# Cross-attention scores with tokens in partitions, probabilities transposed through DRAM, loads in half chunks

## The chip, the cores and the metric

The kernel runs on one core of a Trainium2 chip. The metric is the device time of one execution in microseconds. The core has TensorE (PE; the profile lists its weight loads as PEld), VectorE (DVE), ScalarE (ACT), GpSimd (POOL) and SyncE (SP), each with its own instruction stream, and DMA engines that move data between the on-chip memory (SBUF) and DRAM. Matmuls write to PSUM, which the code divides into banks of 128 x 512 floats.

## The reference

Sixteen sequences of 128 tokens with 512 features go through one block: cross-attention to a context of 2048 rows (without weights), causal self-attention with 16 heads, and a mixture of two of eight low-rank experts chosen by the first token.

```python
def xattn(h, ctx):                       # h: (16, 128, 512), ctx: (16, 2048, 512)
    scores = einsum('bld,bvd->blv', h, ctx)
    probs = softmax(scores, axis=-1)
    return einsum('blv,bvd->bld', probs, ctx)

x = x + xattn(layernorm(x), ctx)
x = x + attn(layernorm(x), Wq, Wk, Wv, Wc)     # 16 heads, rope, causal
x = x + experts(layernorm(x), Wr, A, Bw)       # top 2 of 8, gates from token 0
```

Everything is in float32.

## The kernel before

The program is unrolled over the 16 batches (sequences). For every batch there are four generators, `score`, `attend`, `inner` and `experts`; each `yield` ends one step, and a loop over `b` calls `step(...)` so that the steps of neighbouring batches interleave: while batch `b` is in self-attention (`inner`), the cross-attention of `b + 1` (`attend`) and the scores of `b + 2` (`score`) run, and the experts of `b - 1`. The order on TensorE and the order of the DMAs of `load` are as the program writes them (`keep_in_program_order`); instructions on the other engines may be reordered by the scheduler unless they are `pinned`. The last two batches end in a list, `CLOSING`, that is kept in order on every engine.

All compute instructions of DVE, ACT and POOL pass through one helper and carry the line L115; matmuls are L137, transposes on TensorE L140, pinned DMAs L145. So rows are told apart by tile names.

`score(b)` normalizes `x`, turns it (`hT1`, features in partitions), and multiplies with the transposed context `ctxT`. The context comes in four chunks of 512 rows (VC = 4), each as a transposed copy `ctxT` and a plain copy `ctx`, 1 MB a chunk and copy. With the context chunk as the stationary operand and `hT` as the moving one, the scores `psc` have context rows in partitions: 16 products of 128 x 128 a chunk, four chunks. In float32 the trace has two passes for a product. The maximum over all rows is then one over partitions: elementwise maxima (`mx`), a transpose on TensorE (`tr_m`), a reduction (`nm`), a diagonal matrix (`diag`), a product with ones that spreads it to all partitions (`spread`), four additions on DVE, and four exponentials on ACT. The sums of the probabilities are added up on DVE (`sums`, `part`), and `den` is a product with ones. The probabilities lie as `attend(b)` needs them: context rows in partitions, as the stationary operand against `ctx` (`av`), 16 products of 128 x 512. `x1` is `av` times the inverse sum plus `x`.

`inner(b)` makes v, k and q, the head scores (`pss`), the probabilities in four groups of four heads (`weigh`: mask, peaks, exponentials, scaling), and transposes them by a way through DRAM: DVE transposes blocks of 32 x 32 into `pX`, `send` writes them to DRAM, `fetch` reads them back in the other order into `pT`, from where `y` and then `o` take them. `x2` is `o` plus `x1`. The same way is used for the normalized rows of `score`, `inner` and `experts` (`blocks_1`, `blocks_2`, `blocks_3` to `hT`). All sends and fetches are issued from SP, in program order.

The loads of the loop are issued from ACT's stream, four whole chunks of `ctx` of batch `b + 2` in one place and four of `ctxT` of `b + 3` in another. Each of the two has four buffers, so a chunk's buffer comes free when the chunk of the batch before has been read. PSUM banks: two for scores (`sc`), three for accumulation (`acc`), three for transposes (`tr`).

Of the kernel before, what the change touches and what calls it, by code (L numbers as in the profile page):

```python
# [48 lines left out]
pss0.14 av1.15 m1.14 m0.14 share.13 mx1.14 rx.13 e1.14 lg.13 fold.15 av2.15 choose.13 mx0.14  # L49
ga.13 last_fold.15 e0.14 n1.14 den.15 av3.15 ex.13 n0.14 gb.13 rden.15 gate.13 wa.13 pss1.14  # L50
# [39 lines left out]
def perceiver_block(ctx: ExitStack, tc: tile.TileContext, io: dict, out: bass.AP):  # L90
# [133 lines left out]
    def send(name):  # L224
        if name in ways:
            blocks, dst = ways[name]
            each = blocks.shape[2] * QD
            there = dram.tile([P, 4 * each], F32, tag=f"there_{each}", name=f"there_{name}")
            load(there, blocks.rearrange("p q n j -> p (q n j)"))
            ways[name] = there, dst  # L230

    def fetch(name):
        if name in ways:
            there, dst = ways.pop(name)
            load(
                dst.rearrange("p a n j -> p a (n j)"),
                there.rearrange("(a i) (q e) -> (i q) a e", a=4, q=4),
            )

# [21 lines left out]
    def transposed(src, dst, name, by_tensor):  # L261
        n = src.shape[1] // P
        if by_tensor:
            for piece in tensor_pieces(lambda: src, dst, name, n):
                piece()
        else:
            blocks = p1.tile([P, 4, n, QD], F32, tag=f"blocks_{name[0]}", name=f"blocks_{name}")
            vector.transpose(blocks, src.rearrange("p (n q i) -> p q n i", n=n, q=4))
            ways[name] = blocks, dst
# [74 lines left out]

    def load_ctx(b, vs=range(VC)):
        for v in vs:
            t = p4.tile([P, 4, D], F32, tag="ctx", name=f"ctx_{b}_{v}")

            load(
                t, io["ctx"][b, v * 512 : (v + 1) * 512].rearrange("(p j) d -> p j d", j=4),  # L350
                queue=queue,
            )
            cts.setdefault(b, []).append(t)

    def first_norm(x, hT):

        stats = const.tile([P, 6], F32, name="st_first")
        mv, rstd = const.tile([P, 2], F32, name="mv_first"), const.tile([P, 1], F32, name="rs_first")
        vector.bn_stats(stats, x)
        vector.bn_aggr(mv, stats)  # L360
        pinned(gpsimd.tensor_scalar_add(rstd, mv[:, 1:2], EPS))
        gpsimd.tensor_tensor(rstd, rstd, mhalf, ALU.pow)
        h = p2.tile([P, D], F32, tag="h", name="h_1_0")
        for c in range(KC):

            tr = bank(ps_tr, "tr", f"tr_1_0_{c}") if c else bank(ps_acc, "acc", "tr_1_0_0")
            at = slice(c * P, (c + 1) * P)
            vector.tensor_scalar(
                mixed(h)[:, c], plain(x)[:, c], mv[:, 0:1], rstd, ALU.subtract, ALU.mult
            )  # L370
            transpose(tr[:, :P], h[:, at], ident)
            scalar.copy(hT[:, :, c, :], tr[:, :P].rearrange("p (a j) -> p a j", a=4))
            warm_up(1)


    def score(b):

        hT = p1.tile([P, 4, KC, QD], F32, tag="hT1" if b != 1 else "hT3", name=f"hT1_{b}")
        if b:
            h = layernorm(xs[b], f"1_{b}", mix=b == 1)  # L380
            yield
            transposed(h[:], hT, f"1_{b}", b == 1)
        else:
            first_norm(xs[b], hT)
            yield
        yield

        sc = p2.tile([P, VC, 4, S], F32, tag="sc", name=f"sc_{b}")
        mx = p1.tile([P, 4, S], F32, tag="mx", name=f"mx_{b}")
        for v, ct in enumerate(turned_cts.pop(b)):  # L390
            ps = bank(ps_sc, "sc", f"psc_{b}_{v}").rearrange("p (j t) -> p j t", j=4)
            for j in range(4):

                if v == VC - 1 and j == 3:
                    yield
                for c in range(KC):
                    matmul(
                        ps[:, j, :].rearrange("p (a i) -> p a i", a=4),
                        ct[:, c, j * P : (j + 1) * P], hT[:, :, c, :],
                        start=(c == 0), stop=(c == KC - 1),  # L400
                    )
            scalar.copy(sc[:, v], ps)

            if v:
                vector.tensor_tensor(mx, ps, mx if v > 1 else sc[:, 0], ALU.max)
            if v < VC - 1:
                yield

        def halved(t, op):
            vector.tensor_tensor(t[:, :2], t[:, :2], t[:, 2:], op)  # L410
            vector.tensor_tensor(t[:, 0], t[:, 0], t[:, 1], op)
            return t[:, 0]

        most = halved(mx, ALU.max)
        yield

        tr = bank(ps_tr, "tr", f"tr_m_{b}")
        transpose(tr[:, :S], most, ident)
        nm = p2.tile([P, 1], F32, tag="nm", name=f"nm_{b}")
        vector.tensor_reduce(nm, tr[:, :S], AX.X, ALU.max, negate=True)  # L420
        diag = p1.tile([P, S], F32, tag="diag", name=f"diag_{b}")
        vector.tensor_scalar(diag, ident, nm, None, ALU.mult)
        yield
        spread = bank(ps_tr, "tr", f"spread_{b}")
        matmul(spread[:, :S], ones, diag, start=True, stop=True)
        for v in range(VC):
            vector.tensor_tensor(
                sc[:, v], sc[:, v], spread[:, None, :S].to_broadcast([P, 4, S]), ALU.add
            )
            scalar.activation(sc[:, v], sc[:, v], AF.Exp)  # L430
        part = p2.tile([P, S], F32, tag="part", name=f"part_{b}")
        scores[b] = (sc, part)
        yield
        sums = p1.tile([P, 4, S], F32, tag="sums", name=f"sums_{b}")
        pinned(vector.tensor_tensor(sums, sc[:, 0], sc[:, 1], ALU.add))
        yield
        for v in range(2, VC):
            pinned(vector.tensor_tensor(sums, sums, sc[:, v], ALU.add))

        def fold():  # L440
            vector.tensor_tensor(sums[:, :2], sums[:, :2], sums[:, 2:], ALU.add)

        def last_fold():
            vector.tensor_tensor(part, sums[:, 0], sums[:, 1], ALU.add)

        if b == B - 1:
            named(b, fold=fold, last_fold=last_fold)
        else:
            fold()
            last_fold()  # L450
        yield

    def attend(b):

        sc, part = scores.pop(b)
# [3 lines left out]
        def quarter(v):  # L459
            for j in range(4):  # L460
                matmul(
                    acc, sc[:, v, j, :], ct[v][:, j, :],
                    start=(v == 0 and j == 0), stop=(v == VC - 1 and j == 3),
                )

        state = {}

        def whole():
            den = state["den"] = bank(ps_tr, "tr", f"den_{b}")
            matmul(den[:, :1], part, ones[:, :1], start=True, stop=True)  # L470
# [3 lines left out]
        def inverse():  # L474
            vector.reciprocal(rden[:], state["den"][:, :1])
# [6 lines left out]
        if b == B - 1:  # L482
# [3 lines left out]
                den=whole, rden=inverse, x1=added,  # L486
# [6 lines left out]
        for v in range(VC):  # L493
            quarter(v)
            if v == (VC - 1 if b else VC - 2):
                whole()
                inverse()
# [6 lines left out]
    def inner(b):  # L504
# [167 lines left out]
        def held(chunks=every):  # L672
            acc = banks["y", chunks.start].rearrange("p (c t) -> p c t", c=HC)
            scalar.copy(yT[:, chunks, :], acc[:, chunks, :])
# [98 lines left out]
    def routing(b):  # L773
# [7 lines left out]
            p1, [P, TOP, KC * R], tag="each" if b < B - 1 else "mx", name=f"each_{b}"  # L781
# [54 lines left out]
    def early(b):  # L836
# [22 lines left out]
        row = Later(p1, [P, D], tag="sums", name=f"row_{b}")  # L859
# [12 lines left out]
        def share():  # L872
# [6 lines left out]
            v0s=lambda: summed("v0", "blocks_1"), v0t=value,  # L879
# [9 lines left out]
    def experts(b):  # L889
# [57 lines left out]
        def result(cols=slice(0, D)):  # L947
            vector.tensor_tensor(res[:, cols], banks[cols.start][:, cols], res[:, cols], ALU.add)
# [63 lines left out]
    step(score, 0)  # L1012
    step(score, 1)
    load_weight("v")
    load_weight("k")
    step(attend, 0)
    step(score, 0, 2)
# [5 lines left out]
    step(score, 1)  # L1023
# [15 lines left out]
    for i, n, g in halves:  # L1039
        folded = fold_products(i, n, g)  # L1040
        if ready:
            fold_turned(*ready)
        ready = (n, g, folded)
# [5 lines left out]
    queue = nc.scalar  # L1049
    for b in range(B - 2):  # L1050
        if b + 3 < B:
            load_x(b + 3)
        step(inner, b)
        step(experts, b - 1)
        send(f"3_{b - 1}")
        fetch(f"3_{b - 1}")
# [3 lines left out]
        step(inner, b, 3)  # L1060
        step(score, b + 1, 2)
# [3 lines left out]
        step(inner, b, 2)  # L1065
        step(experts, b - 1)
        step(attend, b + 1)
        step(inner, b)
        step(attend, b + 1)
        step(experts, b - 1)  # L1070
        step(inner, b)
        step(experts, b - 1)
        step(inner, b + 1)
        send(f"p_{b}_0")
        fetch(f"p_{b}_0")
        send(f"p_{b}_1")
        send(f"2_{b + 1}")
        fetch(f"p_{b}_1")
        fetch(f"2_{b + 1}")
        step(score, b + 2, 2)  # L1080
        step(score, b + 3)
        step(score, b + 2)
        load_ctx(b + 2)
        step(score, b + 2)
        step(experts, b - 1)
        step(score, b + 2)
        step(experts, b - 1)
        step(inner, b)
        step(inner, b + 1)
        if b + 3 < B:  # L1090
            load_turned(b + 3)
        step(score, b + 2)
        step(score, b + 3)
        step(inner, b)
        step(score, b + 2)
# [8 lines left out]
    step(score, z, 2)  # L1104
# [54 lines left out]
```

## Time and profile before

| | |
|---|---|
| time, median of 3 runs | 810.63 us (810.39 to 810.79) |
| the profiled execution's own time | 810.97 us |
| its span, first to last instruction | 809.2 us |
| PE busy in the span | 800.2 us (99%) |
| PEld busy | 568.5 us (70%) |
| DVE busy | 529.7 us (65%) |
| ACT busy | 260.4 us (32%) |
| POOL busy | 146.6 us (18%) |
| granted TensorE clock, mean | 0.998 |
| moved by DMA | 211.05 MB, mean 261 GB/s |

"Busy" is the time in which an engine had an instruction in work; matmuls overlap each other, so a busy PE isn't the same as a PE at its peak, and the mean duration of one matmul is longer than the distance from one to the next. A group row reads: line, engine, operation, output and inputs, shape, count, then busy time in all and mean ns of one, then the idle time of the engine just before and what ended it. A timeline row reads: start, duration, engine, line, operation, how many instructions were merged.

### The profile page before, as it was taken

Reading aid. Unit: us, or ns where it says so; the run is one execution under the profiler, and the core shown is the slowest. Engines: PE = TensorE matmul, PEld = TensorE weight load, DVE = VectorE, ACT = ScalarE, POOL = GpSimd, SP = SyncE. Lnnn points to the kernel's source line nnn. Section 1 sums busy time; section 2 is a strip of 40 time slices with the busy share of each in tenths; the row PEclk is TensorE's granted clock in tenths of the full one; section 3 lists DMA queues with packets and bytes.
Section 4 is the critical chain, followed back from the end, with each engine's and each line's share of the span. In section 5 each row is a group of like instructions: output and inputs, shape, how many; then the busy total and the mean of one; then the engine's idle time right before and its main releaser. Section 6 shows DMA issues by size and latency. Waiting matters only on the chain.

```text
span 809.2 us, 14363 instructions
## 1 busy us (share of the span) xinstructions
PE 800.2 (99%) x5538; PEld 568.5 (70%) x5538; DVE 529.7 (65%) x1234; ACT 260.4 (32%) x772; POOL 146.6 (18%) x213
## 2 busy tenths in 40 slices
PE   9999999999999999999999999999999999999996
PEld 9946775768677576866758677676867757686653
DVE  2455759386684947658495775938667584856885
ACT  2232324142232423233241232415223241422461
POOL 1001011212121121211112121111212112121204
PEclk9999999999999999999999999999999999999999
DMA  9998394967849497694958859495885949664102
GB/s 375 417 389 321 118 380 171 340 253 251 360 163 381 172 324 292 221 397 142 364 212 292 320 188 399 152 353 222 281 337 181 388 152 340 261 231 173 41 1 79
DMA packets 76868, 211.05 MB, mean 261 GB/s; under 512 B 6400, under 2 KB 42624, under 8 KB 60416
## 3 DMA queue, kind: packets, MB, share of 16 engines
q10 hardware_dynamic: 15696, 113.32, 35.0%
q1 hardware_dynamic: 57168, 84.75, 29.4%
q0 software_dynamic: 3936, 12.07, 4.4%
q8 instruction: 44, 0.72, 0.3%
q14 instruction: 24, 0.20, 0.1%
HBM read 180.23 MB, written 29.88 MB: 260 GB/s over the span
## 4 chain that ended last, share of the span: by engine, by line
PE 97%; DVE 1%; POOL 0%; issue 0%; ACT 0%; POOLq 0%
PE psc L137 28%; PE av L137 28%; PE k L137 7%; PE q L137 7%; PE v L137 7%; PE o L137 6%; PE pss_sc L137 2%; PE y L137 2%; PE ffn L137 2%; PE pss_acc L137 2%; PE mid L137 2%; PE warm L137 1%; PE tr_m L140 0%; PE tr L140 0%; PE spread L137 0%; PE lg L137 0%
## 5 line engine op out<-in xcount | busy, mean ns | idle before, releaser
L137 PE MATMUL psc<-hT,ctxT 128*128 128x128 f32 x2048 | 235.0, 276 | 0.0
L137 PEld LDWEIGHTS psc<-hT,ctxT 128*128 128x128 f32 x2048 | 231.3, 192 | 0.5 <-issue 0.5
L137 PE MATMUL av<-ctx,sc 128*128 128x512 f32 x512 | 227.3, 596 | 0.0
L137 PEld LDWEIGHTS av<-ctx,sc 128*128 128x128 f32 x512 | 94.4, 190 | 110.5 <-issue 107.9
L115 ACT ACTIVATE att<-att,nmx 128x128 f32<-128x128 f32 x256 | 98.8, 388 | 84.9 <-DVE nmx L115 84.9
L115 POOL TENSOR_SCALAR rs<-mv 128x1 f32<-128x1 f32 x47 | 10.6, 225 | 431.0 <-DVE g_at L115 209.5
L115 ACT COPY sc<-psc 128x512 f32<-128x512 f32 x64 | 37.5, 586 | 140.0 <-PE psc L137 140.0
L115 ACT ACTIVATE sc<-sc 128x512 f32<-128x512 f32 x64 | 40.2, 630 | 90.9 <-DVE sc L115 90.4
L137 PE MATMUL k<-hT,w_k 128*128 128x128 f32 x512 | 60.1, 275 | 0.0
L137 PE MATMUL q<-hT,w_q 128*128 128x128 f32 x512 | 60.0, 275 | 0.0
L137 PEld LDWEIGHTS k<-hT,w_k 128*128 128x128 f32 x512 | 58.5, 192 | 1.5 <-issue 0.8
L137 PE MATMUL v<-w_v,hT 128*32 128x512 f32 x520 | 59.0, 593 | 0.0
L137 PEld LDWEIGHTS q<-hT,w_q 128*128 128x128 f32 x512 | 58.5, 192 | 0.0
L137 PE MATMUL o<-w_c,yT 128*128 128x512 f32 x128 | 57.8, 594 | 0.0
L115 DVE TENSOR_TENSOR mx<-psc,mx 128x512 f32<-128x512 f32 x32 | 21.6, 676 | 55.0 <-ACT sc L115 55.0
L115 ACT ACTIVATE kb<-kT,cst 128x512 f32<-128x512 f32 (+1 forms) x34 | 36.2, 1113 | 39.8 <-DVE kT L115 39.8
L115 DVE TENSOR_SCALAR h<-x,mv,rs 128x512 f32<-128x512 f32 x47 | 27.4, 583 | 31.9 <-POOL rs L115 31.9
L115 ACT ACTIVATION_READ_ACCUMULATOR att<-att,nmx 128x1 f32 x256 | 47.9, 187 | 0.0
L115 DVE TENSOR_TENSOR sc<-sc,spread 128x512 f32<-128x512 f32 x64 | 42.6, 671 | 3.3 <-PE spread L137 3.3
L115 DVE TENSOR_TENSOR att<-att,rsm 128x512 f32<-128x512 f32 x64 | 43.4, 678 | 0.8
L115 DVE TENSOR_REDUCE nmx<-att 128x4 f32<-128x512 f32 x64 | 41.8, 671 | 0.1
L137 PEld LDWEIGHTS o<-w_c,yT 128*128 128x128 f32 x128 | 23.9, 196 | 23.8 <-issue 23.0
(139 smaller groups left out, 851.1 us busy)
## 6 DMA issues: line engine op xcount, KB each, us to landing
ctx<-in_ctx_dram ACTq DMA_DIRECT2D x56, 1024.0 KB, 8.4
ctxT<-in_ctxT_dram ACTq DMA_DIRECT2D x52, 1024.0 KB, 10.5
there_p<-pX SPq DMA_DIRECT2D x28, 512.0 KB, 4.0
pT<-there_p SPq DMA_DIRECT2D x28, 512.0 KB, 4.5
ctxT<-in_ctxT_dram SPq DMA_DIRECT2D x12, 1024.0 KB, 8.9
there<-blocks SPq DMA_DIRECT2D x42, 256.0 KB, 3.3
hT<-there SPq DMA_DIRECT2D x42, 256.0 KB, 3.0
ctx<-in_ctx_dram SPq DMA_DIRECT2D x8, 1024.0 KB, 10.5
```

Source lines behind the costliest of these rows:

```text
L115: ins = issue(*args, **kwargs)
L137: tc.keep_in_program_order(nc.tensor.matmul(*args, **kwargs))
```

## The change

The scores are computed the other way round: `hT1` becomes the stationary operand and the `ctxT` chunk the moving one, so that tokens are in partitions and 512 context rows stream in one matmul; a chunk takes four products of 128 x 512. The maximum is a row maximum (`peaks`, then `nm`), and it enters the exponential as a bias; the exponential gives the row sums (`sums`) too. `mx`, `tr_m`, `diag`, `spread`, the additions, `part` and `den` are gone, and two yields of `score` with them.

The probabilities now lie with tokens in partitions and have to be turned for `attend`. From batch 2 on that goes through DRAM as in `inner`: four DVE transposes into `cX0` and `cX1`, two sends, two fetches into `cT0` and `cT1` (512 KB each). Batches 0 and 1 are turned on TensorE, 16 transposes each, and copied by ACT. `hT1` is laid out so that the column of the stationary operand is every fourth float, `cT` so that it is every eighth. `sc` has one buffer instead of two. `blocks_1` shares its buffer with `cX0`. The host orders the columns of `ctxT` to match.

The loads of the loop are cut into halves (512 KB) and spread over the batch, still on ACT's stream; the steps, sends and fetches are placed anew, `x` is loaded one batch further ahead, and the score of batch 1 is finished in the stage that folds the weights. The copy of `yT`, the last addition of the result, `nm` and the exponentials are pinned; `fold`, `last_fold` and `den` leave `CLOSING`.

```diff
@@ send / fetch
-            each = blocks.shape[2] * QD
+            each = blocks.shape[2] * blocks.shape[3]
+    def by_block(t):
+        return t.rearrange("p a j n -> p a n j")
+    def stationary(t, n):
+        return t[:, :, :, n].rearrange("p a j -> p (a j)")
@@ transposed
-            blocks = p1.tile([P, 4, n, QD], F32, tag=f"blocks_{name[0]}", name=f"blocks_{name}")
-            vector.transpose(blocks, src.rearrange("p (n q i) -> p q n i", n=n, q=4))
+            blocks = p1.tile([P, *dst.shape[1:]], F32, tag=f"blocks_{name[0]}" if name[0] != "1" else "cX0", name=f"blocks_{name}")
+            to = blocks if name[0] != "1" else by_block(blocks)
+            vector.transpose(to, src.rearrange("p (n q i) -> p q n i", n=n, q=4))
@@ loads
+    def load_piece(kind, b, v, half):
+        if b >= B:
+            return
+        chunks, tag = ((cts, "ctx"), (turned_cts, "ctxT"))[kind == "T"]
+        if half == 0:
+            t = p4.tile([P, 4, 512], F32, tag=tag, name=f"{tag}_{b}_{v}")
+            chunks.setdefault(b, []).append(t)
+        of = slice(2 * half, 2 * half + 2)
...
+        load(chunks[b][v][:, of, :], src, queue=nc.scalar)
@@ score
-        hT = p1.tile([P, 4, KC, QD], F32, tag="hT1" if b != 1 else "hT3", name=f"hT1_{b}")
+        hT = p1.tile([P, 4, QD, KC], F32, tag="hT1" if b != 1 else "hT3", name=f"hT1_{b}")
-        sc = p2.tile([P, VC, 4, S], F32, tag="sc", name=f"sc_{b}")
+        sc = p1.tile([P, VC, 512], F32, tag="sc", name=f"sc_{b}")
-            for j in range(4):
-                for c in range(KC):
-                    matmul(
-                        ps[:, j, :].rearrange("p (a i) -> p a i", a=4),
-                        ct[:, c, j * P : (j + 1) * P], hT[:, :, c, :],
-                        start=(c == 0), stop=(c == KC - 1),
-                    )
+            for c in range(KC):
+                matmul(ps, stationary(hT, c), ct[:, c, :], start=(c == 0), stop=(c == KC - 1))
             scalar.copy(sc[:, v], ps)
-            if v:
-                vector.tensor_tensor(mx, ps, mx if v > 1 else sc[:, 0], ALU.max)
+            vector.tensor_reduce(peaks[:, v : v + 1], ps, AX.X, ALU.max)
...
+        pinned(vector.tensor_reduce(nm, peaks, AX.X, ALU.max, negate=True))
...
+        for v in range(VC):
+            pinned(scalar.activation(
+                sc[:, v], sc[:, v], AF.Exp, bias=nm, accum_out=sums[:, v : v + 1]
+            ))
+            vector.transpose(
+                by_block(cX[v // 2])[:, :, v % 2 * 4 : v % 2 * 4 + 4, :],
+                sc[:, v].rearrange("p (n q i) -> p q n i", n=4, q=4),
+            )
+            ways[f"c_{b}_{v // 2}"] = cX[v // 2], cT[v // 2]
@@ attend
-                    acc, sc[:, v, j, :], ct[v][:, j, :],
+                    acc, stationary(cT[v // 2], v % 2 * 4 + j), ct[v][:, j, :],
-            vector.reciprocal(rden[:], state["den"][:, :1])
+            vector.tensor_reduce(rden[:], sums, AX.X, ALU.add)
+            vector.reciprocal(rden[:], rden[:])
@@ inner
-            scalar.copy(yT[:, chunks, :], acc[:, chunks, :])
+            pinned(scalar.copy(yT[:, chunks, :], acc[:, chunks, :]))
@@ the loop over b, as it stands after
         step(inner, b)
         step(experts, b - 1)
         send(f"3_{b - 1}")
         step(inner, b)
         if b:
             load_piece("T", b + 2, 2, 0)
             load_piece("T", b + 2, 2, 1)
         fetch(f"3_{b - 1}")
         if b:
             send(f"1_{b + 2}")
             fetch(f"1_{b + 2}")
         step(inner, b, 2)
         step(attend, b + 1)
         step(inner, b)
         step(attend, b + 1)
         step(inner, b)
         load_piece("C", b + 2, 0, 0)
         if b:
             load_piece("T", b + 2, 3, 0)
         step(inner, b)
         load_piece("C", b + 2, 0, 1)
         send(f"p_{b}_0")
         step(experts, b - 1)
         step(attend, b + 1)
         step(inner, b)
         load_piece("C", b + 2, 1, 0)
         if b:
             load_piece("T", b + 2, 3, 1)
         step(attend, b + 1)
         step(experts, b - 1)
         step(inner, b)
         load_piece("C", b + 2, 1, 1)
         fetch(f"p_{b}_0")
         send(f"p_{b}_1")
         step(experts, b - 1)
         load_piece("C", b + 2, 2, 0)
         step(inner, b + 1)
         send(f"2_{b + 1}")
         step(score, b + 2)
         load_piece("C", b + 2, 2, 1)
         fetch(f"p_{b}_1")
         step(score, b + 2)
         load_piece("C", b + 2, 3, 0)
         fetch(f"2_{b + 1}")
         if b + 4 < B:
             load_x(b + 4)
         step(score, b + 3)
         step(score, b + 2)
         load_piece("C", b + 2, 3, 1)
         step(score, b + 2)
         step(experts, b - 1)
         load_piece("T", b + 3, 0, 0)
         step(score, b + 2, 2)
         step(experts, b - 1)
         send(f"c_{b + 2}_0")
         step(inner, b)
         load_piece("T", b + 3, 0, 1)
         send(f"c_{b + 2}_1")
         fetch(f"c_{b + 2}_0")
         step(inner, b + 1)
         load_piece("T", b + 3, 1, 0)
         load_piece("T", b + 3, 1, 1)
         fetch(f"c_{b + 2}_1")
         step(score, b + 3)
         step(inner, b)
```

## The prediction

> **What bounds the kernel now.** I read the page's busy times and the chain of waits first, then the groups of instructions, then TensorE in order of time through one batch of the loop.
>
> ```profile
> PE 800.2 (99%) x5538; PEld 568.5 (70%) x5538; DVE 529.7 (65%) x1234; ACT 260.4 (32%) x772; POOL 146.6 (18%) x213
> ...
> PE 97%; DVE 1%; POOL 0%; issue 0%; ACT 0%; POOLq 0%
> ```
>
> TensorE (PE) is busy 99% of the span, and the chain that ended last is 97% PE: a microsecond less of matmul is a microsecond less of time, as long as nothing arrives late. The waits list shows next to no idle PE in the loop.
>
> ```profile
> L137 PE MATMUL psc<-hT,ctxT 128*128 128x128 f32 x2048 | 235.0, 276 | 0.0
> L137 PEld LDWEIGHTS psc<-hT,ctxT 128*128 128x128 f32 x2048 | 231.3, 192 | 0.5 <-issue 0.5
> L137 PE MATMUL av<-ctx,sc 128*128 128x512 f32 x512 | 227.3, 596 | 0.0
> L137 PEld LDWEIGHTS av<-ctx,sc 128*128 128x128 f32 x512 | 94.4, 190 | 110.5 <-issue 107.9
> ```
>
> The scores (psc) stream 128 columns a pass, the weighted sum (av) 512. Both do the same arithmetic, but psc loads weights back to back (231.3 us), av's weight load idles more than half the time. Durations overlap, so cost is read from start to start:
>
> ```profile
> 397.72 0.33 PE L140 MATMUL tr_m<-ident,mx 128*128 128x128 f32 x1
> 397.89 3.60 PE L137 MATMUL o<-w_c,yT 128*128 128x512 f32 x8
> 401.32 0.39 PE L137 MATMUL spread<-diag,ones 128*128 128x128 f32 x2
> 401.55 3.74 PE L137 MATMUL k<-hT,w_k 128*128 128x128 f32 x32
> ...
> 408.69 3.60 PE L137 MATMUL av<-ctx,sc 128*128 128x512 f32 x8
> 412.22 1.13 PE L137 MATMUL pss_sc<-kb,qT 64*128 64x256 f32 x8
> ...
> 414.15 10.57 PE L137 MATMUL av<-ctx,sc 128*128 128x512 f32 x24
> 424.55 0.28 PE L137 MATMUL den<-ones,part 128*128 128x1 f32 x2
> 424.69 0.37 PE L137 MATMUL lg<-g_part,ones 128*128 128x8 f32 x2
> 424.92 13.64 PE L137 MATMUL psc<-hT,ctxT 128*128 128x128 f32 x120
> 438.40 1.06 PE L137 MATMUL mid<-hT,wa 128*128 128x128 f32 x8
> ```
>
> A batch takes 47.85 us and PE has no hole in it.
>
> [...] That bears on the new stationary operands, 16 bytes (hT1) and 32 bytes (cT) from column to column. No PE row here shows such a load; ScalarE and VectorE show the like:
>
> ```profile
> 409.08 2.37 ACT L115 ACTIVATE kb<-kT,cst 128x512 f32<-128x512 f32 x2 [2.17 <-DVE kT L115]
> 744.11 1.33 ACT L115 ACTIVATE kb<-kT,cst 128x512 f32<-128x512 f32 x2 [2.18 <-DVE kT L115]
> 800.06 1.08 DVE L115 TENSOR_TENSOR res<-x,h 128x512 f32<-128x512 f32 x1
> ```
>
> The first kb reads every fourth float, the second reads in line: 2.37 against 1.33 us, a factor of 1.78. res with one operand read so takes 1.08 us, elsewhere 0.68: 1.59.
>
> **The change on PE, per batch.** Gone: tr_m 0.17 (397.89-397.72), spread 0.23, den 0.14 = 0.54. The scores become 32 passes of 512 columns. Before: 13.48 for 120 passes and 0.89 for the last eight (391.43 to 392.32 a batch earlier) = 14.37. After, priced by av: 3.53+10.40 = 13.93. Saved 0.44; together 0.98. The strided weight load: at best 190 ns, at worst 190x1.78 = 340, both under the 430 of the matmul that covers them, so nothing; without cover each ns over 430 costs 1,024 passes, 1.0 us.
> Batches 2 to 15: 14 x 0.98 = 13.7. Batches 0 and 1 save 1.96 but transpose probabilities on PE: 32 at 0.1275 (the fold transposes, 8 in 1.02) = 4.1; net +2.1. Without stalls 810.97 - 13.7 + 2.1 = 799.4, against the profiled execution (span 809.2 plus 1.8 around it). The median of the runs is 0.3 lower.
>
> **VectorE and ScalarE.** DVE loses four additions of spread, four of sums and the folds, diag (some 6 us a batch). It gains four row maxima (nearest row: nmx reduce, 0.67, as the maxima removed) and four stream transposes, which write at 32 bytes: between 0.70 (pX) and 1.11 (x1.59); I take 0.9. The exponentials take bias and row sum with them: 0.63 plus some 0.06 = 0.69. ACT issues 16 half loads instead of eight whole ones at 0.5 us each, between its exponentials. Neither engine is the bound; what matters is four chains. I put t=0 at k's first matmul; in the new timing av ends at 23.0, psc at 38.0, y starts at 38.96 (second half 39.41), v at 39.86, o at 43.4, the next k at 46.9.
>
> First, x1. In the changed order DVE meets x1 = av*rden+x, which waits for av's end, ahead of the last group's scaling and its transpose into pX; before, x1 came behind them. So DVE stands from about 21 to 23.2. From x1's start to the norm's end took 2.76 us (425.52 to 428.28); then h 0.52, indices 0.40, blocks 0.61, rows and reciprocal 0.30, scaling 0.68, transpose 0.70: pX is ready at 29.2. The send of p_1 and its fetch follow. The page has medians of 4.0 and 4.5 us: landing at 37.8, 1.6 us before y's second half (more on this below).
>
> Second, the first row maximum queues behind that transpose and four gate instructions (0.45): it ends at 30.25. PE wants that bank for psc's third chunk at 30.16. A late bank also exposes part of the 0.19 weight load. Between 0 and 0.5 us a batch; I take 0.25.
>
> Third, the probabilities. psc ends at 38.0; copy 38.8, maximum 39.5, nm 39.7; four exponentials to 42.5; yT's copy behind them to 43.1, just before o at 43.4. Two transposes to 42.3, send 4.0, fetch 4.5: cT at 51, av wants it at 54.0. 3 us to spare.
>
> Fourth, the LayerNorm's blocks_1 now share cX0's buffer and wait for that send (46.3). Queued behind on DVE: x2, its norm, the shuffle of k. o ends only at 46.9, so the wait is nearly covered; kb is ready at 9.4 of the next batch, pss wants it at 10.7.
>
> SP carries four more DMAs a batch (0.37 us each); p_0's send leaves earlier and the loads come in halves over the batch. Bytes: 211 MB plus 28 x 1.05 = 240, 300 GB/s against slices above 410: room, but the sends meet loads:
>
> ```profile
> 422.67 0.32 SPq L145 DMA_DIRECT2D there_p<-pX  x1
> 425.28 0.37 SPq L145 DMA_DIRECT2D pT<-there_p  x1
> 425.76 0.43 SPq L145 DMA_DIRECT2D there_p<-pX  x1
> ...
> 431.54 0.37 SPq L145 DMA_DIRECT2D pT<-there_p  x1
> ```
>
> SP issues a fetch when its send is done: 2.6 us for p_0 alone, 5.8 for p_1 beside other traffic. [...] Beside the send and fetch of p_1 that stretch of 9 us carries two halves of ctx, hT2 both ways, x and the expert gathers, 3.4 MB or 380 GB/s in all, near the full slices. At 5 and 4.9 us the landing falls on 39.2, a hair ahead of y. I take 0.2 us a batch for y waiting.
>
> Sum of stalls: (0.25+0.2) x 13 = 5.9, and 0.5 for the fold stage, where ACT gains four copies and now waits 0.95 of every 2.04 us. 799.4+6.4 = 805.8 profiled, 805.5 for the median.
>
> **Rivals.**
> Slower: y waits for p_1 every batch. At 5.8 for the send (shown above) and 6.0 for the fetch (its longest landing) pT lands at 29.2+5.8+6.0 = 41.0 against 39.41: 1.6 us x 13 = 21, so about 824 with the other stalls. It decides from send plus fetch of 11.2 us, where the stall eats the 0.98. For it: p_1 was slow before; half loads of ctx now fall into that window. Against: the medians sum to 8.5.
> No stall at all: 799. For it: the first three margins are positive or nearly nothing.
> The weight loads are exposed: from a factor of 2.3 on a load (430/190). At 2.5 (475 ns) 46 us more, about 850. Against: 1.78 is the largest factor seen; for: no PE row.
> No effect: 512 columns save nothing with such loads, and stalls take the 0.54: 808 to 812.
> cT late at av: from 3 us beyond the medians, 815.
>
> **How the numbers follow.** Forecast (801 to 809) 0.48; no stall 0.11; y late 0.27; weights exposed 0.05; cT late 0.04; no effect 0.05. Runs of this kernel tell 0.2%, 1.6 us, from nothing. Faster: 0.48+0.11 and a piece of the last, 0.60; within 0.08; slower 0.32. The range runs from 798.5 to 820: it leaves out the exposed weights and the worse half of the late y, 0.19.
>
> **What would show it.** PE's groups: psc 512 passes at 0.43 us start to start; tr_m, spread and den gone; 32 new transposes. PEld's psc and av rows: up to 340 ns is as argued; above 430 is the rival. A wait of psc's load for DVE peaks of 0.1 to 0.3 us a batch; a wait of y for pT's DMA of some tenths. x1 ahead of the last pX on DVE. A batch of about 47.3 us. Wrong would be a batch above 47.85, with the wait that ends last in y, av or pss.

## The result, and the profile after

The changed kernel takes 908.15 us (median of 4 runs, 901.15 to 912.98) against 810.62 us before (4 runs): a ratio of 1.120, 95% interval 1.112 to 1.127. It is slower by 97.5 us. Forecast were 805.5 us, range 798.5 to 820. Runs of one kernel that lie more than 1.5% above its fastest (one of e2 and three of e12 below) are given, but nothing is concluded from them alone.

The page of the changed kernel, busy times and the first line of the chain that ended last:

```profile
PE 829.6 (91%) x3954; PEld 560.8 (62%) x3954; DVE 514.5 (57%) x1130; ACT 279.6 (31%) x844; POOL 145.7 (16%) x213
...
PE 63%; DMA 24%; DVE 8%; issue 2%; POOL 2%; ACT 0%; SPq 0%; POOLq 0%; DVEq 0%
```

PE's passes have fallen from 5538 to 3954, as forecast, but PE is idle for 9% of the span and the chain is 24% DMA, which had no share in it before.

In what follows a trip is a way through DRAM, and its two legs are the send and the fetch. The trip of p is that of the self-attention's probabilities (`pX` to `pT`, in two halves p_0 and p_1), the trip of c that of the cross-attention's (`cX` to `cT`). The groups of v and y before:

```profile
L137 PE MATMUL v<-w_v,hT 128*32 128x512 f32 x520 | 59.0, 593 | 0.0
...
L137 PE MATMUL y<-pT,vv 128*32 128x128 f32 x512 | 17.5, 276 | 0.0
```

The same groups after, and the DMA issues after (KB each, median us from issue to landing):

```profile
L137 PE MATMUL v<-w_v,hT 128*32 128x512 f32 x520 | 79.0, 761 | 4.2 <-DMA hT<-there 4.2
...
L137 PE MATMUL y<-pT,vv 128*32 128x128 f32 x512 | 23.8, 315 | 50.7 <-DMA pT<-there_p 50.7
```

```profile
there_p<-pX SPq DMA_DIRECT2D x28, 512.0 KB, 7.7
pT<-there_p SPq DMA_DIRECT2D x28, 512.0 KB, 7.3
```

y waits 50.7 us for pT (13 waits of 3.9 us on average), nothing before. The two legs of the trip of p take 7.7 and 7.3 us; before, the medians were 4.0 and 4.5. v, unchanged by the diff, takes 79.0 us instead of 59.0. One batch on PE, in order of time, from psc to the next psc:

```profile
419.11 12.62 PE L137 MATMUL psc<-ctxT,hT 128*128 128x512 f32 x28
433.10 1.16 PE L137 MATMUL mid<-hT,wa 128*128 128x128 f32 x8 [1.37 <-POOL wa L115]
...
441.60 0.90 PE L137 MATMUL y<-pT,vv 128*32 128x128 f32 x16 [4.07 <-DMA pT<-there_p]
442.51 4.98 PE L137 MATMUL v<-w_v,hT 128*32 128x512 f32 x32
...
474.35 1.22 PE L137 MATMUL psc<-ctxT,hT 128*128 128x512 f32 x2
```

The batch is 55.24 us (419.11 to 474.35) against 47.85 before. y's second half waits 4.07 us; mid, the experts' first product, waits 1.37 us for the expert weights, which come by a gather from DRAM. And after the wait the matmuls themselves are slow: v takes 4.91 us from start to start, before 3.54. The windows view names it; its columns are window, length, then busy time of PE, PEld, DVE, ACT and POOL, the granted clock, the DMA share and GB/s:

```profile
436.90:441.60 4.70, 0.63 (x17) 0.36 (x17) 3.73 (x6) 2.93 (x8) 0.00 (x0) 1.00 0.97 293
441.60:447.40 5.80, 5.79 (x48) 1.74 (x48) 2.71 (x5) 0.59 (x1) 0.67 (x1) 0.71 0.93 330
```

PE got 0.71 of its clock in the second window, 1.00 in the one before, in which it waited, and in the one after (447.40 to 450.95). So the stall of this batch is paid twice, 4.07 us of waiting and some 1.8 us of slow y and v (e8 and e9 below show the like behind gaps of 2.35 and 2.93 us).

On SP, the trip of p in that batch:

```profile
415.39 0.33 SPq L145 DMA_DIRECT2D there_p<-pX  x1
423.20 0.36 SPq L145 DMA_DIRECT2D pT<-there_p  x1
425.02 0.33 SPq L145 DMA_DIRECT2D there_p<-pX  x1
...
434.90 0.37 SPq L145 DMA_DIRECT2D pT<-there_p  x1
```

A fetch is issued when its send has landed: 7.8 us for p_0, 9.9 us for p_1, and p_1's fetch lands 6.7 us later. The last pX is ready at 424.99, 6.0 us after av's end. On VectorE the order is indeed the one the prediction saw: x1 and the gate stand ahead of the last scaling and pX.

### The profile page after: what moved, and what is told of

It is laid out like the page before. It is cut to its first block, busy times and chain, and to the rows that moved or that the text cites. A ratio compares the mean times of both kernels' runs of the same rounds, so it can differ in the third digit from the quotient of the medians.

```text
span 908.3 us, 11298 instructions
## 1 busy us (share of the span) xinstructions
PE 829.6 (91%) x3954; PEld 560.8 (62%) x3954; DVE 514.5 (57%) x1130; ACT 279.6 (31%) x844; POOL 145.7 (16%) x213
## 3 DMA queue, kind: packets, MB, share of 16 engines
q10 hardware_dynamic: 31248, 113.33, 38.6%
## 4 chain that ended last, share of the span: by engine, by line
PE 63%; DMA 24%; DVE 8%; issue 2%; POOL 2%; ACT 0%; SPq 0%; POOLq 0%; DVEq 0%
PE av L137 25%; DMA there_p<-pX 9%; PE v L137 9%; DMA pT<-there_p 7%; PE k L137 6%; PE q L137 6%; PE o L137 6%; DMA there<-blocks 4%; PE psc L137 3%; DMA hT<-there 3%; PE pss_sc L137 2%; POOL rs L115 2%; PE pss_acc L137 1%; DVE x L115 1%; DVE st L115 1%
## 5 line engine op out<-in xcount | busy, mean ns | idle before, releaser
L137 PE MATMUL psc<-ctxT,hT 128*128 128x512 f32 x512 | 233.1, 608 | 0.8 <-PE lg L137 0.8
L137 PE MATMUL av<-ctx,cT 128*128 128x512 f32 x512 | 230.7, 603 | 0.0
L137 PEld LDWEIGHTS av<-ctx,cT 128*128 128x128 f32 x512 | 158.2, 315 | 56.6 <-issue 4.6
L137 PEld LDWEIGHTS psc<-ctxT,hT 128*128 128x128 f32 x512 | 154.9, 310 | 60.1 <-DVE peaks L115 6.7
L137 PE MATMUL v<-w_v,hT 128*32 128x512 f32 x520 | 79.0, 761 | 4.2 <-DMA hT<-there 4.2
L115 DVE TENSOR_REDUCE peaks<-psc 128x1 f32<-128x512 f32 x64 | 43.9, 687 | 59.1 <-ACT sc L115 59.0
L137 PE MATMUL y<-pT,vv 128*32 128x128 f32 x512 | 23.8, 315 | 50.7 <-DMA pT<-there_p 50.7
L115 DVE STREAM_TRANSPOSE cX<-sc 128x512 f32<-128x512 f32 x56 | 54.5, 1087 | 13.2 <-ACT sc L115 11.3
L137 PEld LDWEIGHTS y<-pT,vv 128*32 128x32 f32 x512 | 13.9, 121 | 65.3 <-DMA pT<-there_p 54.2
L137 PEld LDWEIGHTS v<-w_v,hT 128*32 128x32 f32 x520 | 20.8, 136 | 51.5 <-issue 49.2
```

The costliest lines, as they stand in the source:

```text
L115: ins = issue(*args, **kwargs)
L137: tc.keep_in_program_order(nc.tensor.matmul(*args, **kwargs))
```

## The experiments

All times are medians, except where a single run or a range is given; the runs of one group share their runs of the kernel before (810.6 to 811.0 us).

| run | edit | us |
|---|---|---|
| e1_whole | whole loads at their old places | 921.3 |
| e2_px_first | last pX ahead of x1 | 908.0 (one run) |
| e3_whole_late | e1, but last pX behind x1 | 919.3 |
| e4_no_c_trip | probabilities' trip left out | 908.3 |
| e5_thin_loads | half loads of 128 KB | 805.0 |
| e10_half_bytes | half loads of 256 KB | 810.0 |
| e6_before_halves | kernel before with half loads | 826.0 |
| e7_placed | whole loads, both moved | 929.7 |
| e8_placed_ctxT | whole loads, ctxT moved | 866.3 |
| e9_own_blocks | e8, blocks_1 out of cX0 | 866.7 |
| e11_one_queue | loads in SP's queue | 850.8 |
| e12_one_queue_spread | e11, spread between the legs | 806.6 to 824.6 |
| e13_one_queue_gather | e12, none beside the gather | 806.6 |
| e14_loads_alone | changed kernel with e13's order of loads and trips | 807.0 |

**Loads, order or volume.** The first theory was that the half loads, spread over the batch, slow the trip of p; the rivals were VectorE's order and the added bytes.

```diff
 # e1_whole: as the kernel before has it
-        load_piece("C", b + 2, 0, 0)
...
-        load_piece("T", b + 3, 1, 1)
+        load_ctx(b + 2)                     # after the third copy of psc
+            load_turned(b + 3)              # after the copy of vv
```

> The changed kernel with its loads as before: four whole chunks of ctx and four of ctxT, at the two places of the loop where the kernel before issues them; all else as changed. With other loads the scheduler also puts the last scaling and its transpose into pX ahead of x1 on VectorE, so this run takes away two suspects at once. Theory 'loads' (the half loads, spread into the stretch where the attention probabilities go to DRAM and back, slow that trip) and theory 'order' (x1 ahead of the last pX makes p_1 late) both expect the stall in y to go: a batch of about 47.0 to 47.8 us, 798 to 812 us in all, sends of p of 2.6 to 4.5 us instead of 7.7. Theory 'volume' (the 29 MB that the probabilities add are what slows everything) expects it to stay above 870 us with sends of p above 6 us.

Measured 921.28 us (919.27 to 922.93). 'Loads' and 'order' were wrong about the time, 'volume' had the time but not the sends: the trip of p is fast again (sends of 2.7 and 5.7 us), and the stall has gone elsewhere. PE of this run, then SP:

```profile
412.23 6.15 PE L137 MATMUL av<-ctx,cT 128*128 128x512 f32 x8 [7.33 <-DVE qP L115]
```

```profile
393.44 2.20 SPq L145 DMA_DIRECT2D there_c<-cX  x2
403.48 4.23 SPq L145 DMA_DIRECT2D cT<-there_c  x2
```

av stands still for 7.33 us. The profile names qP on DVE, which ended 0.35 us earlier, but av doesn't read it; in five other batches it names the landing of cT, and in e3 below DVE was done with q 3 us before av went on. So what comes last is taken to be cT, whose first send took 10 us (393.44 to 403.42). That is the stretch of the old loads: from 384 to 408 DMA is busy all the time (a share of 1.00 to 1.05). The kernel before put its loads where no trip of p lay. The change puts a trip of its own there. (ACT's fourth load of ctxT also left 18 us after its first in this run, about when cT landed, and held kb; no run isolates that.)

```diff
 # e2_px_first: program order, with order edges on VectorE
-        step(attend, b + 1)      # q3 and x1
-        step(experts, b - 1)     # logits, gate
-        step(inner, b)           # weigh 3
+        step(attend, b + 1)      # q3
+        step(inner, b)           # weigh 3, last pX
+        step(experts, b - 1)
+        step(attend, b + 1)      # x1
```

> The changed kernel, half loads and all, with one edit: on VectorE the last reciprocal, scaling and transpose into pX stand ahead of x1 and the gate instructions, as they stood before the change; TensorE's order is the same. The last pX is then ready at about 417.3 on the time axis of the changed kernel's trace instead of 424.99. Theory 'order' expects y's wait (4.07 us a batch) and the slow clock behind it (1.8 us) to go in 13 batches: 825 to 840 us. Theory 'loads' expects little: on SP the send of p_1 stands behind the fetch of p_0, which waits for p_0's slow send until 423.2, so p_1 leaves only some 1.4 us earlier: 13 x 1.4 = 18 less, 880 to 900 us.

Measured 908.0 us (a second run took 923.9): no gain over 908.15, and outside both forecasts. The last pX now is ready at 416.9, but SP holds its send:

```profile
413.53 0.33 SPq L145 DMA_DIRECT2D there_p<-pX  x1
421.52 0.36 SPq L145 DMA_DIRECT2D pT<-there_p  x1
421.98 0.46 SPq L145 DMA_DIRECT2D there_p<-pX  x1
```

p_1's send stands behind p_0's fetch, which waits 8 us for p_0's send; its own landing took 10.8 us more. VectorE's order alone brings nothing. Whether p_1's send ahead of p_0's fetch, with the loads left as they are, would help was not tried.

```diff
 # e3_whole_late: e1 with one order edge (shortened)
+            if group == 3:   # scaling of the last group behind x1
+                tc.add_manual_dep(scaled.ins, ahead[b + 1].ins.name, NO_SYNC)
```

> As the run with whole loads at their old places, but on VectorE x1 and the first gate instructions are held ahead of the last scaling and pX, as in the changed kernel, so the last pX comes some 3 to 6 us after av's end. Theory 'loads' expects a trip of 8 to 10 us for p_1 against about 10 us of room: no wait in y or one of a few tenths, 798 to 815 us. Theory 'order' expects most of the loss to come back: 850 us or more.

Measured 919.26 us, 2 us below e1, with av waiting for the c trip as there and no wait in y. So VectorE's order doesn't decide here either.

```diff
 # e4_no_c_trip
-            ways[f"c_{b}_{v // 2}"] = cX[v // 2], cT[v // 2]
+        scores[b] = kept_cT, sums          # from b = 2 on
```

> The changed kernel without the way of the cross-attention probabilities through DRAM: from batch 2 on nothing of cX is sent or fetched, and av reads the turned probabilities of batch 1 again (this part of the computation is left out); half loads and VectorE's order as changed. 29.4 MB less moved. Theory 'volume' expects the stalls to go: 798 to 820 us. Theory 'loads' expects the sends of p to stay above 6 us and the time above 860 us. Theory 'order' too expects it above 860 us.

Measured 908.3 us (902.7 and 913.9): with 29.4 MB less the time is the same, and y waits 48.5 us for pT. The added volume isn't what makes p late: this run moves 210.85 MB in all, and the kernel before moved 211.05 MB in 810.6 us.

**The bytes of the loads.** What e1 and the changed kernel have in common is that whichever trip lies beside loads is late. To take the bytes away and keep the number of DMAs, their places and their waits:

```diff
 # e5_thin_loads
-            t = p4.tile([P, 4, 512], F32, tag=tag, name=f"{tag}_{b}_{v}")
-            chunks.setdefault(b, []).append(t)
+            chunks.setdefault(b, []).append(present[kind, v])
-        of = slice(2 * half, 2 * half + 2)
+        of = slice(2 * half, 2 * half + 1)
-        load(chunks[b][v][:, of, :], src, queue=nc.scalar)
+        load(chunks[b][v][:, of, :256], src[:, :, :256], queue=nc.scalar)
```

> The changed kernel with each half load of the loop cut from 512 KB to 128 KB, written into the chunk that is already there (so from batch 3 on most of the context is old: this part of the computation is left out); as many loads, in the same places, with the same waits for buffers. Theory 'share' (a trip through DRAM is slow while the bytes of loads are in flight beside it, whichever trip that is) expects sends and fetches of p and c of 2.6 to 4.5 us, no wait in y or av, a batch near 47 us, 794 to 806 us. A theory that the number of DMAs or their waits for one another set the time expects the stalls to stay: above 860 us.

Measured 804.97 us, ratio 0.993 (0.991 to 0.995). Its page, busy times and chain, then the legs of p:

```profile
PE 794.0 (99%) x3954; PEld 556.9 (69%) x3954; DVE 515.1 (64%) x1130; ACT 278.1 (35%) x844; POOL 146.1 (18%) x213
...
PE 96%; DVE 1%; ACT 1%; issue 1%; POOL 1%; POOLq 0%; DVEq 0%; ACTq 0%
```

```profile
there_p<-pX SPq DMA_DIRECT2D x28, 512.0 KB, 3.9
pT<-there_p SPq DMA_DIRECT2D x28, 512.0 KB, 4.6
```

No matmul of the loop waits over 0.7 us any more, with the same 3954 matmuls, the same trips and as many packets in the loads' queue (31248). The two spans give the whole loss: 908.3 - 803.4 = 104.9 us, of which 35.6 is PE busy for longer (829.6 - 794.0; v alone 20.0) and 69.3 idle, 50.7 of it y and 16.1 mid. (The scheduler puts the last pX ahead of x1 here too; e2 shows that this alone brings nothing.)

> The changed kernel with each half load of the loop cut from 512 to 256 KB (again written into chunks already there, so most of the context is old: that part of the computation is left out). A dose between the changed kernel (512 KB: 908 us) and the run at 128 KB (805 us). Theory 'share' expects legs of p of 4.5 to 6 us and, since the trip then ends near the time at which y wants it, 805 to 850 us, nearer to 805.

With 256 KB a half load (`of` one row, 512 columns, 31248 packets again): 809.98 us (18 runs, 807.3 to 812.4), legs of p of 4.9 and 4.7 us, and no matmul of y waits for pT. Half the bytes are still hidden; the loss comes with the other half.

```diff
 # e6_before_halves, in load_turned; load_ctx likewise
-            load(t, io["ctxT"][b, v], queue=queue)
+            for of in (slice(0, 2), slice(2, 4)) if queue is nc.scalar else (slice(0, 4),):
+                load(t[:, of], io["ctxT"][b, v][:, of], queue=queue)
```

> The kernel before with its loads of the loop cut into halves of 512 KB, left in the two places where they were. Theory 'share' expects nothing, since no urgent trip lies beside the loads there: 808 to 814 us. If half loads move their bytes slower by themselves (323 against 400 GB/s of their queue in the two traces) and that is what costs, 820 us or more.

Measured 825.95 us, ratio 1.019 (1.017 to 1.021). The time lies in the range of the second theory, but trips of p are as before (3.8 and 4.5 us), so halving doesn't hurt them where they lie apart from the loads. ACT's stream shows the cost:

```profile
396.57 4.31 ACTq L145 DMA_DIRECT2D ctx<-in_ctx_dram  x8
400.98 0.37 ACT L115 ACTIVATE mid<-mid,g_gate 128x128 f32<-128x128 f32 x1 [3.83 <-DMA ctx<-in_ctx_dram]
```

Eight issues hold ACT for 4.31 us where four took 1.98; mid's copy queues behind them and ffn waits for it, 13.4 us in all. A real cost of halves, but a sixth of the loss, and of another kind.

**Moving the loads.** If sharing is the cause, loads outside both trips should cure it.

```diff
 # e7_placed (with e2's order); in e8 load_ctx stands after the third copy of psc
             fetch(f"1_{b + 2}")
+            load_turned(b + 2)              # after kb
...
         step(score, b + 2)                  # second copy of psc
-        load_piece("C", b + 2, 3, 0)
+        load_ctx(b + 2)
```

> The changed kernel with whole chunks put outside both trips: the four of ctx once p_1's fetch has left (after the second copy of psc), the four of ctxT after kb of the next batch, when c's fetch should have landed; on VectorE the last pX ahead of x1. Same bytes, same trips. Theory 'share' expects most of the stalls to go: sends and fetches of p and c mostly under 5 us, 797 to 825 us. If 14.3 MB a batch are simply too much for DMA, the stall comes up in another place and it stays above 860 us.

> As the run before, but ctx stays at the place it had in the kernel before (after the third copy of psc, 3.5 us later), so its last loads meet c's sends. Theory 'share' expects c's way to be slower than in the run before by some us and, where that passes the slack before av, up to 3 us a batch: 800 to 865 us.

e7 measured 929.7 us, not what 'share' expected but what its rival did, a stall in another place; e8, 3.5 us later with ctx, 866.3, just past its range. In e7 p and c are quick (4.5 to 5.1 us), but the fetches of hT now land 11.2 us after their issue, before 3.0, and v waits 82.7 us for them: the loads had met the next trip in line. (That 240 MB aren't simply too much for DMA is shown by e14.) In e8 VectorE waits 58.4 us for c's send before blocks_1, since blocks_1 lies in cX0; x2, k and q queue behind and pss comes 2.35 us late. After that gap of 2.35 us the granted clock was 0.62 for 4 us (396 to 400).

```diff
 # e9_own_blocks
-  tag=f"blocks_{name[0]}" if name[0] != "1" else "cX0"
+  tag=f"blocks_{name[0]}" if name[0] != "1" else "blocks_2"
...
+            if name[0] == "1":
+                behind(ins, "cX")           # an order edge on VectorE
```

> As the run with ctxT after kb and ctx at its old place, but blocks_1 lies in the buffer of blocks_2 instead of cX0's, so VectorE no longer waits for c's first send (7.3 us, beside the last loads of ctx) before it comes to x2, k and q. If that wait is what makes kb and the head scores late (2.35 us a batch before pss, and a slower clock behind it), the batch falls from 51.3 to about 47 to 47.8 us: 803 to 818 us. If the loads beside c's way delay something else by as much (cT before av, hT1 before psc), it stays above 840 us.

Measured 866.7 us. The wait at blocks_1 went, and hT1, now beside the loads of ctxT, took its place, one of the two delays that the rival named:

```profile
404.84 15.22 PE L137 MATMUL psc<-ctxT,hT 128*128 128x512 f32 x28 [2.93 <-DMA hT<-there]
```

2.93 us of waiting, and the same 28 passes take 15.22 us instead of 12.38 (e8), at a granted clock of 0.50 from 404 to 408 us and 0.65 from 408 to 412. In all the placements tried with whole loads on ACT's queue another trip lay beside them.

**One queue.** In the runs up to here the loads of the loop went out in ACT's queue and the legs in SP's. The next runs rest on an assumption of the author that no trace here shows by itself: a leg in the loads' own queue would wait for what stands ahead of it and for nothing issued later, and the order could be written down.

> The changed kernel with its loads on SP's stream and queue instead of ACT's, as whole chunks in program order between the trips: two of ctx after hT2's fetch, one each behind blocks_1's send and fetch (which now follow c's), one of ctxT behind blocks_3's send and three behind its fetch; on VectorE the last pX ahead of x1, blocks_1 in blocks_2's buffer. Same bytes, same trips. If loads hurt a trip [...], a trip in one queue with the loads waits at most for the one chunk that stands ahead of it (2.6 us at 400 GB/s), and each leg is then short again: 803 to 825 us. If what counts is only that bytes and trips share the time, wherever they are queued, some trip is late again: above 840 us.

Measured 850.77 us, ratio 1.048: the range of the rival. The trace shows a bad order: p_0's send was issued 3 us behind three chunks of ctxT and took 10.8 us, and from 392 to 404 us DMA was busy only 0.34 to 0.78 of the time. That fits a leg that waits for what stands ahead of it; the next run tests it.

> As the run with all loads on SP's queue, with the chunks placed anew, so that never more than one (1 MB) stands ahead of a leg of a trip: one of ctx behind each of p_0's send and p_0's fetch, p_1's send ahead of p_0's fetch, two of ctx and one of ctxT behind hT2's fetch, one of ctxT each behind blocks_1's send, blocks_3's send and hT3's fetch. In the run before, p_0's send stood behind three chunks and took 10.8 us, while DMA was busy only 0.34 to 0.78 in the 12 us after it. If a leg's delay is the bytes ahead of it in its queue, the legs of p fall to 3 to 6 us and y's wait goes: 803 to 820 us. If the order within the queue does not matter, it stays near 850 us.

Measured 806.6, 813.4 and 814.5 us, and in three more runs 818.9 to 824.6; the profiled one, the fastest, has no stall in y, v or av. What the others wait for, no profile shows; the gather was closest to late.

> As the run with loads in SP's queue, never more than one chunk ahead of a leg, but the chunk of ctx that stood between p_0's and p_1's fetch goes behind hT2's fetch, so no load lies beside the expert gather; blocks_3's send goes ahead of hT1's fetch and of one chunk of ctxT. If the gather was what made executions differ (806.6 to 824.6 us), they now lie together at 803 to 811 us. If it was another leg, the spread stays above 10 us.

Measured 806.57 us (805.1 to 807.7), ratio 0.9945 (0.993 to 0.996). The spread is gone; since blocks_3's send and hT1's fetch moved too, that it was the gather isn't shown.

```diff
 # e14_loads_alone, against the changed kernel (conditions left out)
         send(f"3_{b - 1}")
+            fetch(f"1_{b + 2}")
+            load_turned(b + 2, [1])
...
         fetch(f"3_{b - 1}")
-            send(f"1_{b + 2}")
-            fetch(f"1_{b + 2}")
+            load_turned(b + 2, [2, 3])
...
         send(f"p_{b}_0")
+        load_ctx(b + 2, [0])
...
+        send(f"p_{b}_1")
         fetch(f"p_{b}_0")
-        send(f"p_{b}_1")
...
         fetch(f"2_{b + 1}")
...
+        load_ctx(b + 2, [1, 2, 3])
...
         fetch(f"c_{b + 2}_1")
         step(score, b + 3)
+        send(f"1_{b + 3}")
+            load_turned(b + 3, [0])
         step(inner, b)
@@ and the sixteen half loads of a batch
-        load_piece("C", b + 2, 0, 0)
...
-        load_piece("T", b + 3, 1, 1)
```

> The changed kernel with the loads (and the sends and fetches of hT1 and p_1 among them) in SP's queue in the order of the run beside it, and no other edit: no order forced on VectorE, blocks_1 in cX0's buffer as the change has it. If the loads are the whole cause: within 4 us of the run beside it, 803 to 814 us. If blocks_1's wait for c's send (4.5 us in the last profile, ending about when o does) costs by itself, 1 to 2 us a batch more: 815 to 835 us.

Measured 807.02 us (805.6 to 808.3), ratio 0.9952 (0.994 to 0.997): 3.9 us (0.5%) faster than the kernel before, with all of the change's arithmetic, bytes and trips; the legs of p have medians of 4.9 and 5.9 us. The edit is the loads, whole, in SP's queue and in this order, with p_1's send and hT1's trip placed among them; VectorE's order follows from it, since the scheduler puts the last pX ahead of x1 again. One batch on PE of this run:

```profile
388.85 1.05 PE L137 MATMUL mid<-hT,wa 128*128 128x128 f32 x8
...
392.53 1.08 PE L137 MATMUL y<-pT,vv 128*32 128x128 f32 x32
393.43 3.62 PE L137 MATMUL v<-w_v,hT 128*32 128x512 f32 x32
...
423.90 4.66 PE L137 MATMUL psc<-ctxT,hT 128*128 128x512 f32 x10
```

No idle in brackets, and psc began at 376.63: a batch of 47.27 us. What the one queue, the order, the whole chunks and p_1's earlier send are worth apart isn't shown: the same order with the loads on ACT's queue wasn't tried.

## Why the prediction was wrong

**The step that failed** is the one on DMA: "Bytes: 211 MB plus 28 x 1.05 = 240, 300 GB/s against slices above 410: room, but the sends meet loads". Room in the mean was read as room for a trip, and legs of 5 and 4.9 us for p_1 gave the term that was far too small, "0.2 us a batch for y waiting". Measured: legs of 9.9 and 6.7 us in the batch shown, and 3.9 us a wait, 50.7 us in all. The medians of 4.0 and 4.5 us were measured where no load of the context was in flight; with a half load issued every few microseconds they were 7.7 and 7.3 (e5 has them at 3.9 and 4.6, by taking only bytes away). The slices above 410 GB/s weren't what DMA moves beside a trip: from 419.1 to 441.6 us, around the trip of p_1, it was busy 0.82 to 0.97 of the time and moved 291 to 299 GB/s. The queues' busy shares add up to 77.7% of 908.3 us, 706 us of DMA time, which is 88% of an execution of 800 us, not the 73% of 300 in 410; before it was 69.2% of 809.2, 560 us. In e14 the same bytes take 661 us and no matmul of the loop waits over 0.7 us: in the sum there was room, beside that trip there wasn't. The loads' queue moved 323 GB/s (113.33 MB in 38.6% of 908.3 us), before 400.

**The rival "y late"** had the place and the sign right and too small a price: 5.8 and 6.0 us for the legs of p_1, 1.6 us of waiting, where 3.9 us were measured. It also priced a stall only once; the slower matmuls behind it add half as much again (35.6 us to 69.3). And it left out that the gather is slow beside loads too (its median from issue to landing is 7.3 us, before 3.2): mid's 16.1 us stood in none of the cases.

**The arithmetic on PE held.** Its sums come out to within 0.1 us; psc has 512 passes; tr_m, spread and den are gone; e14 makes the batch in 47.27 us, forecast 47.3. But that agreement is luck, since two errors cancel in the number. The forecast without stalls was 47.85 - 0.98 = 46.87. The missing 0.40 lies in the products whose weight load is strided, costed at nothing: the load takes 310 to 315 ns on average against 190, under the matmul, as argued, and yet in e14 24 passes of av take 10.53 us instead of 10.40, eight 3.66 instead of 3.53, psc 14.06 instead of 13.93. The 0.45 of stalls that filled the gap in the forecast aren't in e14. That is some 6 ns a pass, 64 passes a batch; that the stride is its cause is argued, not shown by a run.

**x1 ahead of pX** was seen rightly (pX at 6.0 us after av's end, forecast 6.2) and blamed too much: e2 undoes it and gains nothing; there SP sends p_1 behind p_0's fetch. The prediction looked at VectorE's queue and not at that one.

**cT** was given 3 us to spare and had them in the changed kernel, where av waits for nothing; in e1, with the loads of the kernel before, it was the stall. **blocks_1** behind cX0's send, "nearly covered", was so in the changed kernel (13.8 us of VectorE's waiting in all) until the send met loads (58.4 us in e8). **VectorE's transposes** took 1.09 us on average against 0.9 taken, near the upper bound of 1.11; no wait of a matmul is put down to them. An exponential took 0.71 us from start to start, the reading of its row sum included, against 0.69. **The late bank** was met: psc's weight load waits for the row maxima 12 times, 0.56 us on average, and the 28 passes of the batch shown take 12.62 us against 12.38 in e14, where no such wait is listed: 0.24 us, 0.25 taken. **The start** cost 3.0 us by v of batch 0 (67.86 against 64.83) where 2.6 were forecast.

## What to carry to other kernels

Price a trip through DRAM by what else is in flight beside it, not by its median and not by the mean GB/s: the same 240 MB took 908 us in one order and queue and 807 us in another. When a change adds a trip, list every trip of the loop and every stretch with bulk loads: here moving loads away from one trip put them beside the next, and only fewer bytes or another order helped. The order that did: bulk loads in the queue of the trips, at most one chunk close ahead of an urgent leg, two or three only where the next leg left 7 to 10 us later.

## What was not expected of the hardware

With the same half loads at 128, 256 and 512 KB the kernel takes 805, 810 and 908 us: the loss isn't proportional to the bytes; that it sets in where the slack of a trip ends fits the legs of p (3.9, 4.9 and 7.7 us for the send). After a gap of 2.35 us the granted clock was 0.62 for 4 us (e8), after one of 2.93 us 28 passes of psc took 2.84 us longer (e9). In e11 two gaps of 0.97 and 1.29 us with 0.64 us of y between them were followed by 5.15 us of v instead of 3.54, with a clock of 0.57 from 408 to 412 us, while the fourteen waits of ffn in e6, 0.96 us on average, left the mean clock at 0.998. And with all bulk loads in one queue the chip moved the same 240 MB at 298 GB/s over the span without a stall above 0.7 us in the loop, with DMA busy for 82% of it (e14).
